# First aggregation of a graph attention layer: both outer strips of scores in one turning product, h's 64-column rests turned in pairs, the first group's h turned ahead of the next sums

## The chip, the cores and the metric

The kernel runs on one core of one Trainium2 chip. The time is device microseconds of one execution. Before the change three runs took 1733.44, 1734.93 and 1737.89 us; the median is 1734.93 us.

## What is computed

Two layers of relational graph attention over 3125 nodes and 53125 edges (sorted by their target), with 768 features; the first layer has 4 heads of 192 columns, the second one head of 768. Then a residual and a normalisation. Cut to what matters:

```python
def rgat_conv(x, W, q, k, b, src, dst, etype, heads, out_ch, n_nodes):
    xr = jnp.einsum('nd,rdf->rnf', x, W)          # 3 relations
    oi = xr[etype, dst]
    oj = xr[etype, src]
    alpha = jax.nn.leaky_relu(oi @ q + oj @ k, NEG_SLOPE)
    m = jax.ops.segment_max(alpha, dst, num_segments=n_nodes)
    e = jnp.exp(alpha - m[dst])
    z = jax.ops.segment_sum(e, dst, num_segments=n_nodes)
    a = e / (z[dst] + EPS)
    msg = (a[:, :, None] * oj.reshape(-1, heads, out_ch)).reshape(-1, heads * out_ch)
    return jax.ops.segment_sum(msg, dst, num_segments=n_nodes) + b

h = jax.nn.elu(rgat_conv(x, W1, q1, k1, b1, src, dst, edge_type, 4, 192, n))
out = rgat_conv(h, W2, q2, k2, b2, src, dst, edge_type, 1, 768, n)
x = _layernorm(x + out, axis=-1)
```

## The kernel before, in words

The work has three stages, one after another. `phase1` (with the preparation ahead of it) multiplies x by W1 for all relations and stores the rows, each with its key score, in a table in memory. `phase2` is the first aggregation: it gathers the rows of the table edge by edge, weighs and adds them per target node, makes h from the sums, multiplies h by W2 and stores the rows of the second table. `phase3` is the second aggregation over that table, with the residual and the normalisation.

Both aggregations take the nodes in 25 groups of 128. A group has 17 slots (14 in the first group) of 128 edges. One slot is one indirect DMA issued by GpSimd (`gather_rows`, L480), which brings 128 rows of 772 floats into a ring of row buffers. The slots 0 to 7 of a group are its first part (u = 0), the others its second (u = 1).

One part of a group in `phase2` runs through these steps. `alpha` (L887) adds the query and key scores of the part's slots and takes the leaky maximum into `al`, one column for each slot and head, with 128 edges down the partitions. `turn` (L898) turns these columns into rows in PSUM, three times by three products of TensorE: the slots shifted back by one, the slots themselves, the slots shifted on by one. The three strips of 128 columns stand side by side in the bank `pa`. `scan` (L906) needs the middle strip and 64 columns (`REACH`) on either side of it: two running maxima on VectorE, a difference, and an exponential on ScalarE. `back` (L919) turns the result back, `weigh` (L940) multiplies it into the selection matrices `sel`, and `sums` (L957) adds the rows by products with `sel` into two banks `acc`.

Once for each group come the steps of h. `e_y` (L1001) divides by the sum of weights and adds the bias, giving `y` (four windows of 192 columns, in a tile whose windows are 256 wide); `e_x` takes the exponential on ScalarE; `e_h` (L1051) finishes the elu in three VectorE steps, of which one puts the last 64 columns of each window a second time behind the 192, so that each window has two blocks of 128. `h_row` stores h. `e_t` (L1066) turns y by eight products into the PSUM tile `pt`: `turned(s, 0)` the first 128 columns of the four windows, `turned(s, 1)` the last 128, which hold the same 64 columns twice. `e_s` copies the high parts into `hT` on ScalarE (one copy of 512 columns, two of 256 on 64 partitions each), and `e_s2` makes the low parts on VectorE in the same pieces. `d_part` issues the 72 products of h with W2 one by one, `d_row` (L1102) copies each quarter of the result out and, after every second quarter, stores a whole row block of 386 KB.

`phase3` does the same with one head: `a_alpha` (L1294), `a_turn` (L1304, again three products), `a_scan`, and so on.

The order on every engine is written out by hand. Each step is given a place, counted in slots, by `when(place, step, ...)`, and all steps are issued in the order of their places. `STEPS2["h"]` holds the places of e_y, e_x, e_h, h_row, e_t, e_s and e_s2, `STEPS2["first"]` and `STEPS2["second"]` those of alpha, turn, scan, back, weigh and sums of the two parts. For the first group (b = 0) the base is -3, for the second 14; a group's base is that of the one before plus 17. A gather also waits for a product of the group before, by a count of TensorE cycles (`paced`, L489).

Of the kernel before, what the change touches and what calls it, by code (L numbers as in the profile page):

```python
# [21 lines left out]
P = 128  # L22
# [8 lines left out]
REACH = 64  # L31

# [32 lines left out]
def _index(ap):  # L65
# [4 lines left out]
SL = 17  # L70
# [21 lines left out]
          "h": (26.1, 26.45, 28.4, 28.5, 34.52, 34.6, 34.62),  # L92
          "d": ((37, 38.5, 16), (43.2, 45.2, 20), (45.5, 47, 16), (51.7, 53.7, 20)),
# [21 lines left out]
def kernel(  # L115
# [355 lines left out]

    W3 = P + 2 * REACH

# [365 lines left out]
    def phase2(work, psum):  # L839
# [15 lines left out]
        for t in als:  # L855
            V.memset(t, 0.0)
# [30 lines left out]
        def alpha(b, u):  # L887
            if u == 0:
                st["a", b] = work.tile([P, SL, H1], F32, name="a", bufs=2)
            a = st["a", b]  # L890
            i, e = (0, CUT + 1) if u == 0 else (CUT + 1, slots(b))
            for i_, e_, g in stretches(ring, lambda j: base(b) + j, i, e):
                key = g.rearrange("p n (h f) -> p n h f", h=H1)[:, :, :, F1]
                V.tensor_add(a[:, i_:e_], pall[:, b, i_:e_], key)
                V.memset(key, 1.0)
            V.scalar_tensor_tensor(als[b % 2][:, 1 + i:1 + e], a[:, i:e], NEG_SLOPE, a[:, i:e], op0=ALU.mult, op1=ALU.max)

        def turn(b, u):  # L898
            a, e = part(b, u)
            n = H1 * (e - a)  # L900
            pa = st["pa", b, u] = psum.tile([P, 512], F32, name=f"pa{u}", bufs=1)
            for c in range(3):
                T.transpose(pa[:n, c * P:(c + 1) * P],
                            als[b % 2][:, a + c:e + c].rearrange("p j h -> p (j h)"), ident)
# [96 lines left out]
        def e_y(b):  # L1001
# [6 lines left out]
            y = s["y"] = work.tile([P, 4, 2 * P], F32, name="y", bufs=1)  # L1008
            for w in range(4):
                V.scalar_tensor_tensor(y[:, w, :F1], acc[w // 2][:, w % 2, :F1], rz[:, w // 2, w % 2:w % 2 + 1],  # L1010
                                       bias1, op0=ALU.mult, op1=ALU.add)

        def e_x(b):
            s = blk[b]
            s["ey"] = work.tile([P, 4, F1], F32, name="ey", bufs=1)
            S.activation(s["ey"], s["y"][:, :, :F1], AF.Exp)
# [7 lines left out]
        def turned(s, c):  # L1024

            for t in range(4):
                T.transpose(s["pt"][:, c, t * P:(t + 1) * P], s["y"][:, t, c * P:(c + 1) * P], ident)

        def high_parts(s, c):
# [6 lines left out]
            for u in range(2):  # L1036
                p = slice(64 * u, 64 * u + 64)
                S.copy(hT[p, 0, H1:], pt[p, u::2])

        def low_parts(s, c):  # L1040
# [6 lines left out]
            for u in range(2):  # L1047
                p = slice(64 * u, 64 * u + 64)
                V.tensor_sub(hT[p, 1, H1:], pt[p, u::2], hT[p, 0, H1:].bitcast(F32))

        def e_h(b):  # L1051
# [3 lines left out]
            V.scalar_tensor_tensor(y[:, :, F1:], y[:, :, P:F1], 0.0, ey[:, :, P:], op0=ALU.max, op1=ALU.add)  # L1055
            V.scalar_tensor_tensor(y[:, :, :F1], y[:, :, :F1], 0.0, ey, op0=ALU.max, op1=ALU.add)

        def h_row(b):
# [4 lines left out]
            for h in range(H1):  # L1063
                nc.sync.dma_start(to[h], s["y"][32 * h:32 * h + 32, :, :F1])
# [37 lines left out]
        def d_row(b, p):  # L1102
# [5 lines left out]
            if c == 1:  # L1108
# [27 lines left out]
        for b in range(NB):  # L1136
# [14 lines left out]
            for d, f in zip(STEPS2["h"], (e_y, e_x, e_h, h_row, e_t, e_s, e_s2)):  # L1151
                when(at_0 + d, f, b)
# [22 lines left out]
    def phase3(work, psum):  # L1175
# [7 lines left out]
        for t in als:  # L1183
# [110 lines left out]
        def a_alpha(b):  # L1294
# [7 lines left out]
            V.scalar_tensor_tensor(al[:, 1:SL + 1], a, NEG_SLOPE, a, op0=ALU.mult, op1=ALU.max)  # L1302

        def a_turn(b):  # L1304
            pa = blk[b]["pa"] = psum.tile([P, 512], F32, name="pa", bufs=1)
            for c in range(3):
                T.transpose(pa[:SL, c * P:(c + 1) * P], als[b % 2][:, c:c + SL], ident)
# [892 lines left out]
```

## Time and profile before

| what | value |
| --- | --- |
| three runs | 1733.44, 1734.93, 1737.89 us |
| the profiled execution's own time | 1735.37 us |
| its span, first to last instruction | 1733.4 us |
| TensorE busy | 1643.7 us, 95% |
| weight loads | 1277.1 us, 74% |
| VectorE busy | 1075.3 us, 62% |
| ScalarE busy | 423.3 us, 24% |
| GpSimd busy | 910.8 us, 53% |
| mean granted TensorE clock | 0.977 of full speed |
| moved by DMA | 500.48 MB |

All times inside the profile are microseconds from the span's start unless they are marked ns. PE is TensorE, PEld its weight loads, DVE VectorE, ACT ScalarE, POOL GpSimd, SP SyncE; a q behind the name is the engine's own queue. L58 is the line of a helper that records every turning product and L55 that of every other product, so the tiles tell them apart: `pa` is the bank of the scores, `pt` that of h, `acc` the sums, `po` the products with W2, `hT` the turned h. In a row of the timeline the first number is the start, the second the length, and xN the number of instructions merged into it; what stands in brackets is the idle time of the engine just before and what ended it. In the chain of waits, the piece ahead of each line is what held up the work that ended last.

The first aggregation lies between about 534 and 1131 us, the second between about 1135 us and the end.

### The profile page before, as it was taken

Reading aid. Unit: us, or ns where it says so; the run is one execution under the profiler, and the core shown is the slowest. Engines: PE = TensorE matmul, PEld = TensorE weight load, DVE = VectorE, ACT = ScalarE, POOL = GpSimd, SP = SyncE. Lnnn points to the kernel's source line nnn. Section 1 sums busy time; section 2 is a strip of 40 time slices with the busy share of each in tenths; the row PEclk is TensorE's granted clock in tenths of the full one; section 3 lists DMA queues with packets and bytes.
Section 4 is the critical chain, followed back from the end, with each engine's and each line's share of the span. In section 5 each row is a group of like instructions: output and inputs, shape, how many; then the busy total and the mean of one; then the engine's idle time right before and its main releaser. Section 6 shows DMA issues by size and latency. Waiting matters only on the chain.

```text
span 1733.4 us, 39074 instructions
## 1 busy us (share of the span) xinstructions
PE 1643.7 (95%) x14308; PEld 1277.1 (74%) x14308; DVE 1075.3 (62%) x3953; ACT 423.3 (24%) x796; POOL 910.8 (53%) x907
## 2 busy tenths in 40 slices
PE   9999999999996999999999999939999999999996
PEld 8999999999995788888888888924444444444443
DVE  5467666675425556665677777455666666666665
ACT  5122222112110111111111111202333333333333
POOL 5100000000007777777777777067777777777770
PEclk9999999999997999999999999969999999999999
DMA  9676766666568999999999999579999999999990
GB/s 328 185 237 211 256 218 212 198 179 211 197 236 290 342 342 343 349 347 341 341 352 351 355 348 343 163 235 321 335 337 336 333 339 333 339 335 338 334 329 29
DMA packets 169367, 500.48 MB, mean 289 GB/s; under 512 B 39890, under 2 KB 82489, under 8 KB 169166
## 3 DMA queue, kind: packets, MB, share of 16 engines
q0 software_dynamic: 70832, 343.91, 56.1%
q1 hardware_dynamic: 90104, 143.89, 25.0%
q10 hardware_dynamic: 8230, 10.10, 1.7%
q8 instruction: 114, 1.87, 0.4%
q14 instruction: 87, 0.71, 0.1%
HBM read 412.96 MB, written 89.63 MB: 290 GB/s over the span
## 4 chain that ended last, share of the span: by engine, by line
PE 74%; DMA 11%; issue 6%; POOL 4%; DVE 3%; ACT 0%; POOLq 0%; SPq 0%; DVEq 0%; ACTq 0%
PE po L55 45%; PE acc L55 17%; PE D L55 6%; DMA waL<-ftab,ridx 3%; DMA waH<-ftab,ridx 3%; PE pa L58 2%; POOL waH L480 2%; PE pt L58 1%; DMA share<-ftab,ridx 1%; POOL waL L480 1%; DMA share<-in_w_t_dram 1%; POOL extra L480 1%; DMA extra<-ftab,rfirst 1%; DMA e<-in_edge_type_dram 1%; DMA extra<-ftab,ridx 1%
## 5 line engine op out<-in xcount | busy, mean ns | idle before, releaser
L480 POOL DMA_INDIRECT extra<-ftab,ridx x296 | 305.8, 1033 | 90.2 <-issue 53.3
L55 PE MATMUL po<-waH,hT 128*128 128x386 f32 (+1 forms) x1200 | 322.7, 344 | 1.0 <-DVE hT L1045 0.8
L55 PE MATMUL po<-waH,xT 128*128 128x386 f32 x1104 | 293.0, 341 | 0.0
L480 POOL DMA_INDIRECT share<-ftab,ridx x209 | 216.4, 1036 | 63.7 <-issue 36.6
L55 PEld LDWEIGHTS po<-waH,hT 128*128 128x128 f32 x1200 | 220.1, 189 | 3.4 <-DVE hT L1045 1.1
L55 PE MATMUL po<-waL,hT 128*128 128x386 f32 (+1 forms) x600 | 207.5, 346 | 0.0
L55 PE MATMUL D<-extra,AT 128*128 128x512 f32 (+1 forms) x576 | 203.3, 504 | 0.0
L55 PEld LDWEIGHTS po<-waH,xT 128*128 128x128 f32 x1104 | 202.5, 189 | 0.5 <-issue 0.4
L55 PE MATMUL po<-waL,xT 128*128 128x386 f32 x552 | 186.9, 339 | 0.0
L55 PEld LDWEIGHTS D<-extra,AT 128*128 128x128 f32 x576 | 108.3, 195 | 79.5 <-issue 73.5
L593 ACT COPY share<-po 128x386 f32<-128x386 f32 x150 | 72.4, 483 | 371.4 <-PE po L55 303.9
L55 PE MATMUL acc<-waL,marks 128*32 128x386 f32 (+1 forms) x860 | 151.9, 489 | 0.0
L55 PE MATMUL po<-wbH,xT 128*128 128x386 f32 (+1 forms) x552 | 147.4, 341 | 1.3 <-DVE wbL L430 1.3
L55 PE MATMUL acc<-waH,marks 128*32 128x384 f32 (+1 forms) x828 | 140.4, 493 | 0.7 <-DVE marks L1346 0.7
L55 PE MATMUL acc<-extra,marks 128*32 128x386 f32 (+1 forms) x564 | 129.5, 487 | 0.0
L480 POOL DMA_INDIRECT waL<-ftab,ridx x108 | 108.1, 1001 | 32.9 <-issue 27.4
L55 PE MATMUL acc<-extra,sel 128*32 128x193 f32 x2736 | 123.2, 332 | 2.2 <-DVE sel L953 2.2
L917 ACT ACTIVATE e<-e 32x128 f32<-32x128 f32 (+2 forms) x50 | 15.5, 310 | 436.2 <-DVE e L916 436.2
L480 POOL DMA_INDIRECT waH<-ftab,ridx x103 | 104.0, 1010 | 31.4 <-issue 26.2
L55 PEld LDWEIGHTS po<-waL,hT 128*128 128x128 f32 x600 | 113.4, 189 | 0.6 <-issue 0.3
L757 POOL DMA_DIRECT2D share<-in_L_gnn_W_dram x24 | 12.9, 538 | 188.4 <-DVE w2j L768 117.2
L55 PEld LDWEIGHTS acc<-extra,sel 128*32 128x32 f32 x2736 | 86.7, 111 | 32.0 <-issue 6.7
(302 smaller groups left out, 3045.0 us busy)
## 6 DMA issues: line engine op xcount, KB each, us to landing
ftab<-share SPq DMA_DIRECT2D x150, 193.0 KB
ftab<-r SPq DMA_DIRECT2D x50, 386.0 KB
sT<-dr_d SPq DMA_DIRECT2D x23, 544.0 KB
xb_d<-share SPq DMA_DIRECT2D x25, 384.0 KB
ftab<-y SPq DMA_DIRECT2D x100, 96.0 KB
share<-xb_d SPq DMA_DIRECT2D x25, 384.0 KB
share<-in_x_dram SPq DMA_DIRECT2D x24, 384.0 KB
out_dram<-share SPq DMA_DIRECT2D x24, 384.0 KB
```

The costliest lines, as they stand in the source:

```text
L55: return self.add(self.engine.matmul(to, weights, moving, **more), to, moving)
L58: return self.add(self.engine.transpose(to, a, unit), to, a)
L480: return G.indirect_dma_start(out=to, out_offset=None, in_=tab, in_offset=_index(i[:, j:j + 1]), bounds_check=NP * R - 1, oob_is_err=False)
L593: S.copy(o[:, :HW], po[:, :HW])
L757: G.dma_start(w2[i][p:p + n], l2["W"][r, at:at + n, :])
L917: S.activation(e, e, AF.Exp)
```

## The change

In both aggregations the two outer strips are made by one turning product in place of two. A new tile (`near`, in the second aggregation `next_to`) gets, by two VectorE copies of 64 partitions each, the edges 0 to 63 of the next slot and the edges 64 to 127 of the slot before; its product writes two blocks of 64 columns to either side of the middle strip, through the view `sides`. `alpha` and `a_alpha` gain the two copies, `turn` and `a_turn` have two products in place of three.

The last 64 columns of h's windows go into a tile of their own, `rest`, four times 64 columns, and are turned two windows at a time: two products in place of four. `y` has windows of 192 columns with no gap. `e_s` and `e_s2` take the rests in four pieces of 128 columns on 64 partitions in place of two of 256.

The first group has its own places, `h0`: e_h 0.08 of a slot earlier, e_t, e_s and e_s2 1.32 to 1.38 slots earlier. In the last group `d_row` stores each quarter by itself.

```diff
+    def sides(pa):
+        return pa[:, P - REACH:P - REACH + 2 * (P + REACH)].rearrange("n (s f) -> n s f", s=2)[:, ::-1, :REACH]
...
           "h": (26.1, 26.45, 28.4, 28.5, 34.52, 34.6, 34.62),
+          "h0": (26.1, 26.45, 28.32, 28.5, 33.2, 33.22, 33.24),
...
+            al, to = als[b % 2], near[b % 2]
+            n = max(i, 1)
+            V.tensor_copy(to[:REACH, n - 1:e - 1], al[:REACH, 1 + n:1 + e])
+            n = min(e, SL - 1)
+            V.tensor_copy(to[P - REACH:, 1 + i:1 + n], al[P - REACH:, 1 + i:1 + n])
 
         def turn(b, u):
...
-            for c in range(3):
-                T.transpose(pa[:n, c * P:(c + 1) * P],
-                            als[b % 2][:, a + c:e + c].rearrange("p j h -> p (j h)"), ident)
+            T.transpose(pa[:n, P:2 * P], als[b % 2][:, 1 + a:1 + e].rearrange("p j h -> p (j h)"), ident)
+            T.transpose(sides(pa[:n]), near[b % 2][:, a:e].rearrange("p j h -> p (j h)"), ident)
...
-            for t in range(4):
-                T.transpose(s["pt"][:, c, t * P:(t + 1) * P], s["y"][:, t, c * P:(c + 1) * P], ident)
+            if c == 0:
+                for t in range(4):
+                    T.transpose(s["pt"][:, 0, t * P:(t + 1) * P], s["y"][:, t, :P], ident)
+                return
+            for t in range(2):
+                T.transpose(s["pt"][:, 1, t * P:(t + 1) * P], s["rest"][:, t * P:(t + 1) * P], ident)
+
+        def rests(s, k):
+            hT = s["hT"].rearrange("p s t (m q i) -> p s t m q i", q=2, i=32)
+            pt = s["pt"][:, 1, :2 * P].rearrange("p (m t u i) -> p t m u i", m=2, u=2, i=32)
+            for u in range(2):
+                for q in range(2):
+                    yield hT[64 * u:64 * u + 64, k, H1:, :, q], pt[64 * q:64 * q + 64, :, :, u]
...
-            for u in range(2):
-                p = slice(64 * u, 64 * u + 64)
-                S.copy(hT[p, 0, H1:], pt[p, u::2])
+            for to, rest in rests(s, 0):
+                S.copy(to, rest)
...
-            for u in range(2):
-                p = slice(64 * u, 64 * u + 64)
-                V.tensor_sub(hT[p, 1, H1:], pt[p, u::2], hT[p, 0, H1:].bitcast(F32))
+            for (to, rest), (high, _) in zip(rests(s, 1), rests(s, 0)):
+                V.tensor_sub(to, rest, high.bitcast(F32))
...
-            V.scalar_tensor_tensor(y[:, :, F1:], y[:, :, P:F1], 0.0, ey[:, :, P:], op0=ALU.max, op1=ALU.add)
-            V.scalar_tensor_tensor(y[:, :, :F1], y[:, :, :F1], 0.0, ey, op0=ALU.max, op1=ALU.add)
+            V.scalar_tensor_tensor(s["rest"].rearrange("p (w f) -> p w f", w=4), y[:, :, P:], 0.0, ey[:, :, P:], op0=ALU.max, op1=ALU.add)
+            V.scalar_tensor_tensor(y, y, 0.0, ey, op0=ALU.max, op1=ALU.add)
...
-            if c == 1:
+            if b == NB - 1:
+                f = slice(c * HW, (c + 1) * HW)
+                nc.sync.dma_start(s["rows"][:, r, f], rows[r][:, f])
+            elif c == 1:
                 nc.sync.dma_start(s["rows"][:, r, :], rows[r])
...
-            for d, f in zip(STEPS2["h"], (e_y, e_x, e_h, h_row, e_t, e_s, e_s2)):
+            for d, f in zip(STEPS2["h" if b else "h0"], (e_y, e_x, e_h, h_row, e_t, e_s, e_s2)):
...
+            V.tensor_copy(next_to[b % 2][:REACH, :SL - 1], al[:REACH, 2:SL + 1])
+            V.tensor_copy(next_to[b % 2][P - REACH:, 1:], al[P - REACH:, 1:SL])
...
-            for c in range(3):
-                T.transpose(pa[:SL, c * P:(c + 1) * P], als[b % 2][:, c:c + SL], ident)
+            T.transpose(pa[:SL, P:2 * P], als[b % 2][:, 1:SL + 1], ident)
+            T.transpose(sides(pa[:SL]), next_to[b % 2], ident)
```

More of the change, by code (lines that the diff above doesn't have):

```diff
@@ L31 @@
 REACH = 64
+assert 2 * REACH == P
 GRP = 8
@@ L854, in phase2 @@
         als = [work.tile([P, SL + 2, H1], F32, name=f"al{i}", bufs=1) for i in range(2)]
-        for t in als:
+        near = [work.tile([P, SL, H1], F32, name=f"near{i}", bufs=1) for i in range(2)]
+        for t in als + near:
             V.memset(t, 0.0)
@@ L1007, in e_y @@
             V.reciprocal(rz, rz)
-            y = s["y"] = work.tile([P, 4, 2 * P], F32, name="y", bufs=1)
+            y = s["y"] = work.tile([P, 4, F1], F32, name="y", bufs=1)
+            s["rest"] = work.tile([P, 2 * P], F32, name="rest", bufs=1)
             for w in range(4):
-                V.scalar_tensor_tensor(y[:, w, :F1], acc[w // 2][:, w % 2, :F1], rz[:, w // 2, w % 2:w % 2 + 1],
+                V.scalar_tensor_tensor(y[:, w], acc[w // 2][:, w % 2, :F1], rz[:, w // 2, w % 2:w % 2 + 1],
                                        bias1, op0=ALU.mult, op1=ALU.add)
@@ L1015, in e_x @@
             s["ey"] = work.tile([P, 4, F1], F32, name="ey", bufs=1)
-            S.activation(s["ey"], s["y"][:, :, :F1], AF.Exp)
+            S.activation(s["ey"], s["y"], AF.Exp)
         def busy(n):
@@ L1063, in h_row @@
             for h in range(H1):
-                nc.sync.dma_start(to[h], s["y"][32 * h:32 * h + 32, :, :F1])
+                nc.sync.dma_start(to[h], s["y"][32 * h:32 * h + 32])
         def e_t(b):
@@ L1182, in phase3 @@
         als = [work.tile([P, SL + 3], F32, name=f"al2_{i}", bufs=1) for i in range(2)]
-        for t in als:
+        next_to = [work.tile([P, SL], F32, name=f"next{i}", bufs=1) for i in range(2)]
+        for t in als + next_to:
             V.memset(t, 0.0)
```

## Prediction

> **What bounds the kernel now.** I read the page first, then the busy time by stretches, the chain of waits, the waits of TensorE, and the timelines of single engines.
>
> ```profile
> PE 1643.7 (95%) x14308; PEld 1277.1 (74%) x14308; DVE 1075.3 (62%) x3953; ACT 423.3 (24%) x796; POOL 910.8 (53%) x907
> ```
>
> 95% is an average over stages, so the stages are looked at one by one. First one group of the first aggregation. Columns: stretch, length, busy time (and instructions) of PE, PEld, DVE, ACT, POOL, granted clock, DMA share, GB/s.
>
> ```profile
> 850.40:873.40 23.00, 23.00 (x276) 19.86 (x280) 15.12 (x48) 4.26 (x10) 17.81 (x18) 1.00 0.98 343
> ```
>
> TensorE has no gap and the full clock; the waits of TensorE between 600 and 1080 us list nothing. The chain of waits gives the period, from the second part's sums of two groups:
>
> ```profile
> 597.36 4.38 PE acc L55 x104
> ...
> 1103.32 4.38 PE acc L55 x104
> ```
>
> 22 groups lie between them: (1103.32 - 597.36) / 22 = 23.00 us each. The second aggregation's gathers, the first and the last of 422:
>
> ```profile
> 1135.47 1.21 POOL L480 DMA_INDIRECT waH<-ftab,rfirst  x1 [47.49 <-DMA f<-ed_d]
> 1687.27 1.00 POOL L480 DMA_INDIRECT share<-ftab,ridx  x1 [0.30 <-issue]
> ```
>
> 421 steps in 551.8 us are 1.31 us each, which is one gather (1.00) and its issue (0.30 to 0.31) with next to nothing between. So the first aggregation lasts as long as TensorE's work, and the second starts when the first ends and then lasts as long as GpSimd issues gathers.
>
> **Turning products.** TensorE at the two places in a group where parts are turned:
>
> ```profile
> 854.71 0.50 PE L58 MATMUL pa<-fident,al 128*32 128x128 f32 x3
> ...
> 865.28 0.50 PE L58 MATMUL pa<-fident,al 128*36 128x128 f32 x3
> 865.62 1.04 PE L58 MATMUL pt<-fident,y 128*128 128x128 f32 x8
> 866.41 0.42 PE L55 MATMUL po<-waL,hT 128*128 128x386 f32 x1
> ```
>
> Starts count here, not lengths, since products overlap. Three products on `al` take 865.62 - 865.28 = 0.34 us, 0.113 each; eight on y take 866.41 - 865.62 = 0.79, 0.099 each. A group loses two of the first kind (one in each part) and two of the second: 0.226 + 0.198 = 0.42 us. The new product writes two blocks of 64 columns, a shape that no row shows; I take the price of one plain product, since it moves as many columns. Cheaper it could only be by the 0.113 itself; as two pieces of 0.113 it would take back that edit's gain. From 578 to 1131 us 46 parts and 24 groups' y are turned: 46 x 0.113 + 48 x 0.099 = 9.9 us, if nothing else becomes late.
>
> **What is late next: the gathered rows.** VectorE's `alpha` waits for them, and the turning products wait for `alpha`.
>
> ```profile
> 601.14 0.18 DVE L896 SCALAR_TENSOR_TENSOR al<-a 128x36 f32<-128x36 f32 x1
> 601.67 0.50 PE L58 MATMUL pa<-fident,al 128*32 128x128 f32 x3
> ...
> 876.88 0.22 DVE L894 TENSOR_TENSOR a<-pall,share 128x32 f32<-128x32 f32 x1 [1.61 <-DMA share<-ftab,ridx]
> 877.17 0.16 DVE L896 SCALAR_TENSOR_TENSOR al<-a 128x36 f32<-128x36 f32 x1
> 877.70 0.50 PE L58 MATMUL pa<-fident,al 128*32 128x128 f32 x3
> ...
> 1083.11 0.18 DVE L896 SCALAR_TENSOR_TENSOR al<-a 128x36 f32<-128x36 f32 x1
> 1084.63 0.50 PE L58 MATMUL pa<-fident,al 128*32 128x128 f32 x3
> ```
>
> The first part's `al` is ready 0.35 us ahead of its turning at 601 and 0.37 at 877; over the 13 groups from the one to the other it is 0.15 to 0.87, 0.57 in the mean. The change draws on this twice. Two copies come between `al` and the turning product: 0 to 0.18 us each, by the step before them, and the first waits for that step's result; 0.1 to 0.4 together, I take 0.25, the middle. And TensorE comes 0.31 us sooner (one strip and two y products lie between the point that sets the gathers' pace and this turning). Taking 0.56 from each of the 13 leaves six below zero, 1.4 us in sum. Behind the product that then waits a group's 20 `po` products are queued, so such a wait is the path's.
>
> What sets the gathers' pace, VectorE first, then GpSimd:
>
> ```profile
> 860.42 0.55 DVE L1053 TENSOR_SCALAR ey<-ey 128x768 f32<-128x768 f32 x1
> 861.01 0.42 DVE L1055 SCALAR_TENSOR_TENSOR y<-y,ey 128x256 f32<-128x256 f32 x1
> 861.47 0.96 DVE L1056 SCALAR_TENSOR_TENSOR y<-y,ey 128x768 f32<-128x768 f32 x1
> ...
> 861.54 1.75 POOL L480 DMA_INDIRECT share<-ftab,ridx  x1 [0.30 <-PE po L55]
> 863.60 1.00 POOL L480 DMA_INDIRECT share<-ftab,ridx  x1 [0.30 <-DVE moved L986]
> ...
> 1086.98 1.00 POOL L480 DMA_INDIRECT share<-ftab,ridx  x1 [0.30 <-issue]
> ```
>
> The gather that begins under `e_h`'s last step ends 0.86 us after it, 0.75 late. 17 gathers and their issue are 22.2 us, with this one hold 23.0: it ties the gathers to TensorE's period, and at 22.58 us need only be 0.4 long. From 863.60 on the steps that move the index hold gathers too: 166 gathers in 223.38 us are 22.88 us a group. Against 22.58 they lose 0.30 a group. The slack there (1.34 us at 1084), less 0.56, carries about three of ten groups; seven lose 0.30, 2.1 us. The first aggregation keeps 9.9 - 1.4 - 2.1 = 6.4 us.
>
> The Trainium skill ("SBUF — State Buffer", "Who interferes with whom") says that a VectorE copy can enter a mode that takes the port pair shared with GpSimd, and that whichever of the two comes second is blocked for the whole instruction. The held gather agrees in kind; no run here shows it of such copies. By the rows alone the copies hold nothing and the sum stands; by the rule at its full reach it would be that of the slower rival below.
>
> **h's high and low parts.** ScalarE, VectorE, and TensorE's first use:
>
> ```profile
> 868.18 0.74 ACT L1038 CAST hT<-pt 64x256 fp32r<-64x256 f32 x2
> 868.95 0.69 DVE L1045 TENSOR_TENSOR hT<-pt,hT 128x512 fp32r<-128x512 f32 x1 [1.55 <-ACT hT L1038]
> 869.56 0.85 DVE L1049 TENSOR_TENSOR hT<-pt,hT 64x256 fp32r<-64x256 f32 x2
> 870.29 0.44 PE L55 MATMUL po<-waH,hT 128*128 128x386 f32 x1
> ```
>
> Four pieces of half the size cost between the same and double, 0.74 to 1.48 and 0.85 to 1.70; I take 1.1 on both, nearer the same. The first low part, which waits for all the high ones, ends at 869.64 and would come 0.36 later; TensorE needs it 0.31 sooner, with the third product, a little after 870.29. Of 0.7 us or more of cover some remains. It costs nothing, at the dear end about 0.4 a group.
>
> **The first group.** e_h moves ahead of the next group's `weigh` on VectorE; the turning of y, and its split on ScalarE and VectorE, ahead of that group's sums. GpSimd's queue has one gather between, which waits for none of this; SP's has nothing. (The row from 572 is one of stretches; its clock is 0.50.)
>
> ```profile
> 559.15 0.84 ACT L1016 ACTIVATE ey<-y 128x768 f32<-128x768 f32 x1 [1.41 <-DVE y L1010]
> 559.03 1.54 DVE L953 TENSOR_TENSOR sel<-marks,pa 128x1024 f32<-128x1024 f32 x2
> 560.29 5.46 PE L55 MATMUL acc<-extra,sel 128*32 128x193 f32 x80 [2.19 <-DVE sel L953]
> 570.11 0.62 PE L55 MATMUL po<-waH,hT 128*128 128x386 f32 x2 [0.75 <-DVE hT L1045]
> 572.00:574.00 2.00, 2.00 (x7) 1.56 (x5) 1.97 (x10) 0.00 (x0) 1.70 (x2) 0.50 0.91 358
> 574.01 1.14 PE L55 MATMUL acc<-extra,sel 128*32 128x193 f32 x16
> ```
>
> This is a new wait: VectorE stands until ScalarE's exponential ends at 559.99, then does e_h's three steps, to 562.0. `sel` is queued behind it and the sums wait for `sel`, so they come 2.9 us later, at 563.2. They take 5.5 us as before, or 3.4 at the second part's full pace (80 of 104 in 4.38). In return the products that stood until 570.11, 4.4 us after the sums, no longer wait for the split: 0.74 + 0.69 us less, 2.9 after. They are 16, at half clock 4.5 us (14 took 3.9), at full clock 2.3. The next sums begin between 571.8 and 576.1, against 574.01; I take no change, the middle.
>
> **The end of the stage, and the rest.**
>
> ```profile
> 1131.92 2.60 DMA ftab<-r
> ```
>
> The last store, on which the second aggregation's gathers wait, is halved: 0 to 1.3 us less, I take 0.5, nearer to a fixed price as no split store is shown. The copies on the path at the start and in the last groups cost 0.3 (0.25 less one strip, each), and 50 of them beside the second aggregation's gathers another 0.3: +0.6. One strip less in each group there gives nothing, as GpSimd sets its length.
>
> **Sum.** -6.4 - 0.5 + 0.6 = -6.3 us. The profiled execution took 1735.4, so 1729.1; the median of the runs is 0.4 below that execution: 1728.7.
>
> **Rivals.**
> 1. The whole 9.9 us arrives, because the landings come sooner too (for it: 1.34 us of slack at 1084; against: six of 13 slacks below zero): -9.9 - 0.5 + 0.6, 1725.2. Chance 0.19.
> 2. The landings set the period and it stays at 23.0 (for it: DMA share 0.98; against: GpSimd's 22.2): +0.1, 1735.1. Chance 0.16.
> 3. The two blocks of 64 cost two products, so that edit does not do what it says: 5.2 us go, and most of the waits with them; 1730.9. Chance 0.1.
> 4. Slower: each copy holds a gather for its length. Its place is the second aggregation, where GpSimd has no cover: 50 x 0.18 = 9 us; in the first, four copies a group bring the gathers to 22.9, so 2 of the 9.9 remain. 1742. It decides from 0.13 us per copy, where 50 of them eat 6.5. Against it: 421 steps there hold only 2.4 us in all beyond 1.305 each. Chance 0.05.
>
> The forecast has 0.50. A measurement of this kernel can tell about 0.3%, 5.2 us, from no change, so faster begins below 1729.7: some 0.37 of the forecast and rival 1, 0.56. Slower is rival 4, 0.05; the same 0.39. The range, 1724.0 to 1733.8, goes a little below rival 1 and takes in rival 3 and the dear ends of the forecast; it leaves out rivals 2 and 4, 0.2.
>
> **What would show it.** Right: 22.6 to 22.8 us between the sums; two `pa` and six `pt` products at 0.10 to 0.11 from start to start; waits of TensorE at `pa` for VectorE's copies, 0.1 to 0.3 a group; the second aggregation's gathers 551 to 553 us from first to last; a last store under 2.6. A period of 22.58 without such waits is rival 1, one of 23.0 rival 2, 0.2 us behind the new product rival 3, long gathers beside copies rival 4. I am wrong if the period falls and the time does not.

## The result, and the profile after

Nine runs of the changed kernel took 1730.03 us in the median (1727.71 to 1733.77), nine runs of the kernel before beside them 1735.03 (1733.44 to 1738.55). The ratio is 0.9969 (95% interval 0.9960 to 0.9979): 5.0 us less, where 6.3 were forecast. The profiled execution took 1729.88 us, its span is 1728.1.

The page of the changed kernel, the line of busy times:

```profile
PE 1636.1 (95%) x14183; PEld 1266.2 (73%) x14183; DVE 1113.7 (64%) x4157; ACT 431.5 (25%) x846; POOL 906.0 (52%) x907
```

TensorE has 125 recorded products and 7.6 us less, VectorE 204 instructions and 38.4 us more. What that is worth shows only stage by stage. First the two turning places of one group on TensorE, for which the starts count:

```profile
853.17 0.28 PE L59 MATMUL pa<-fident,al 128*32 128x128 f32 x1
853.29 0.27 PE L59 MATMUL pa<-fident,near 128*32 128x128 f32 x1
...
863.66 0.29 PE L59 MATMUL pa<-fident,al 128*36 128x128 f32 x1
863.79 0.27 PE L59 MATMUL pa<-fident,near 128*36 128x128 f32 x1
863.90 0.60 PE L59 MATMUL pt<-fident,y 128*128 128x128 f32 x4
864.33 0.38 PE L59 MATMUL pt<-fident,rest 128*128 128x128 f32 x2
864.47 0.42 PE L56 MATMUL po<-waL,hT 128*128 128x386 f32 x1
```

The product of the two blocks of 64 columns takes 0.11 us (863.79 to 863.90), as much as a plain one, and the whole place 0.81 us where it took 1.13. Now the chain of waits, sums of the second part, four groups in a row:

```profile
848.85 4.38 PE acc L56 x104
871.46 4.38 PE acc L56 x104
894.01 4.38 PE acc L56 x104
917.12 4.55 PE acc L56 x104
```

The period is 22.61 and 22.55 us: 0.42 less than the 23.00 of before, to the digit of the forecast. The last one is 23.11, and its sums take 4.55 us in place of 4.38. Such longer periods are the largest part of the difference between the 9.9 us that the products gave and the 5.0 that came. The waits of TensorE between 600 and 1130 us (total, times, longest), name some of them (the list counts only idle stretches of over 0.15 us); before the change this list is empty:

```profile
PE pa L59 <- DVE al L903: 2.1, 4, 0.9
PE acc L56 <- DVE sel L964: 1.5, 3, 0.5
PE pa L59 <- DVE near L908: 0.3, 1, 0.3
```

Shorter waits for the copies show only from start to start. Where the scores came late, as at the longest of these waits, the product on `near` follows the one on `al` after 0.31 us in place of 0.12:

```profile
762.68 0.27 PE L59 MATMUL pa<-fident,al 128*32 128x128 f32 x1 [0.86 <-DVE al L903]
762.99 0.28 PE L59 MATMUL pa<-fident,near 128*32 128x128 f32 x1
```

Between group 3 and group 24 this happens at six turnings of first parts, 0.20 to 0.55 us each, together 1.3 us more than 0.12 each.

The end of the stage, from the chain of waits, and the first and the last of the second aggregation's 422 gathers:

```profile
1128.88 1.87 DMA ftab<-r
```

```profile
1131.53 0.99 POOL L486 DMA_INDIRECT waH<-ftab,rfirst  x1 [45.09 <-DMA ftab<-r]
...
1681.05 1.00 POOL L486 DMA_INDIRECT share<-ftab,ridx  x1 [0.30 <-issue]
```

The last store takes 1.87 us in place of 2.60, the second aggregation begins 3.9 us sooner (1.0 of it because group 0 was turned that much sooner in this execution), and its gathers take 549.5 us from first to last (551.8 before).

For all kernels below I use one table. It cuts the profiled execution at the turning of the first part of group 0, of group 3 and of group 24, at the first gather of the second aggregation, and at the last one (us; each number is the difference of two starts in the timeline).

| kernel | group 0 to 3 | 3 to 24 | 24 to first gather | these three | gathers |
| --- | --- | --- | --- | --- | --- |
| before | 61.1 | 483.0 | 50.8 | 594.9 | 551.8 |
| before, second profile | 62.0 | 483.6 | 50.9 | 596.5 | 550.2 |
| after | 62.6 | 480.1 | 49.3 | 592.0 | 549.5 |
| after, second profile | 65.1 | 476.3 | 49.3 | 590.6 | 549.8 |
| e_h in four | 62.9 | 476.8 | 49.3 | 589.0 | 548.9 |
| first part turned later | 65.3 | 479.2 | 48.4 | 592.8 | 551.2 |
| first h not ahead | 61.4 | 477.1 | 49.3 | 587.7 | 549.1 |
| three mends | 61.3 | 474.7 | 49.3 | 585.3 | 549.9 |
| strips alone | 61.6 | 481.0 | 50.6 | 593.3 | 551.1 |
| rests alone | 62.0 | 481.5 | 50.5 | 593.9 | 551.2 |

From group 3 to group 24 are 21 groups; at 22.57 us, the mean of the undisturbed ones, they take 474.0. The profile of after lies 6.1 us above that, its second profile 2.3. The two profiles of one kernel differ by 1.4 to 1.6 us over the three stretches, so smaller differences between kernels can't be read from this table.

### The profile page after: what moved, and what is told of

Same layout as the page of the kernel before. It is cut to its first block, busy times and chain, and to the rows that moved or that the text cites. A ratio compares the mean times of both kernels' runs of the same rounds, so it can differ in the third digit from the quotient of the medians.

```text
span 1728.1 us, 39081 instructions
## 1 busy us (share of the span) xinstructions
PE 1636.1 (95%) x14183; PEld 1266.2 (73%) x14183; DVE 1113.7 (64%) x4157; ACT 431.5 (25%) x846; POOL 906.0 (52%) x907
## 4 chain that ended last, share of the span: by engine, by line
PE 68%; DMA 13%; issue 7%; DVE 6%; POOL 4%; ACT 0%; POOLq 0%; DVEq 0%; ACTq 0%; SPq 0%
PE po L56 44%; PE acc L56 13%; PE D L56 6%; DMA extra<-ftab,ridx 4%; DMA waL<-ftab,ridx 2%; DMA share<-ftab,ridx 2%; PE pa L59 2%; DMA waH<-ftab,ridx 2%; POOL waH L486 2%; PE pt L59 1%; DMA spare_rows<-ftab,ridx 1%; POOL waL L486 1%; POOL extra L486 1%; POOL share L486 1%; DVE marks L1374 1%
## 5 line engine op out<-in xcount | busy, mean ns | idle before, releaser
L56 PE MATMUL acc<-share,marks 128*32 128x384 f32 (+1 forms) x456 | 109.7, 487 | 0.0
## 6 DMA issues: line engine op xcount, KB each, us to landing
sT<-dr_d SPq DMA_DIRECT2D x23, 544.0 KB
```

The source lines that it names most:

```text
L56: return self.add(self.engine.matmul(to, weights, moving, **more), to, moving)
```

## The experiments

**On a slower chip.** The first four kernels ran on another chip, on which the kernel before takes 1948.32 us (1947.35 to 1952.82). My theory A was that the step of e_h that holds a gather ties the gathers to TensorE's pace; B that the rows land late because the DMA queues are full; C that the copies of the scores cost what is missing.

e_h's last step in four:

```diff
-            V.scalar_tensor_tensor(y, y, 0.0, ey, op0=ALU.max, op1=ALU.add)
+            for w in range(4):
+                V.scalar_tensor_tensor(y[:, w], y[:, w], 0.0, ey[:, w], op0=ALU.max, op1=ALU.add)
```

> The changed kernel with e_h's last step (0.96 us) cut into four steps of one window each. Theory A (the gathers run at TensorE's pace because that step holds one of them until it ends, so a group that comes sooner gets its rows no sooner): holds of at most 0.3 us, the gathers run ahead, 22.5 to 22.7 us from one first-part turning to the next in nearly all groups, waits of TensorE in groups 3 to 24 of 2 us or less against 7.7 us in the changed kernel, 1724 to 1726.5 us. Theory B (the DMA queues are full, the rows land late whatever GpSimd does): waits stay at 5 to 8 us, 1729 to 1731. Theory C (the new copies cost the time, by their length or by holding gathers): no change, 1729 to 1731, with long gathers beside the copies.

Measured: 1964.80 us, ratio 1.0085 (1.0067 to 1.0102).

The rows of h not stored, x's rows copied into the table during the first stage:

```diff
+            if b < NB - 1:
+                return
             for h in range(H1):
                 nc.sync.dma_start(to[h], s["y"][32 * h:32 * h + 32])
```

> The changed kernel without the stores of h's rows in the first aggregation (384 KB of some 7.8 MB a group; x's rows stand in the table in their place, copied during the first stage). Theory B: 5% less to move, the DMA share falls to about 0.93, the landings come sooner, waits of 2 us or less, 1724 to 1727. Theories A and C: waits stay at 5 to 8 us, 1728.5 to 1731.

Measured: 1963.76 us, ratio 1.0079 (1.0065 to 1.0093).

Only the strips of scores, in both aggregations, with their copies; the rest as before:

```diff
-            for c in range(3):
-                T.transpose(pa[:n, c * P:(c + 1) * P], ...)
+            T.transpose(pa[:n, P:2 * P], als[b % 2][:, 1 + a:1 + e].rearrange("p j h -> p (j h)"), ident)
+            T.transpose(sides(pa[:n]), near[b % 2][:, a:e].rearrange("p j h -> p (j h)"), ident)
...
```

> Only the turning products of the scores are changed (both aggregations, with the copies); h's rests, the first group's places and the stores are those of before. Theories A and B: a saving of 0.226 us a group draws little on the slack, waits of 1 to 2 us, 1730.5 to 1732.5. Theory C: the copies eat the saving, 1734 to 1736.

Measured: 1958.37 us, ratio 1.0048 (1.0034 to 1.0062).

Only h's rests; the scores, the places and the stores as before:

```diff
-                T.transpose(s["pt"][:, c, t * P:(t + 1) * P], s["y"][:, t, c * P:(c + 1) * P], ident)
+            for t in range(2):
+                T.transpose(s["pt"][:, 1, t * P:(t + 1) * P], s["rest"][:, t * P:(t + 1) * P], ident)
...
```

> Only h's rests are changed (two products fewer a group, four half-size pieces in place of two); scores, places and stores are those of before, no copies. Theories A and B: 0.2 us a group, nearly all kept, 1730.5 to 1732. Theory C: the same, and all that the whole change gains, 1729.5 to 1731, while the strips alone gain nothing.

Measured: 1958.79 us, ratio 1.0052 (1.0038 to 1.0066).

Here nothing could be told apart, because another thing sets the time. Busy time by stretches on this chip, e_h in four, and below it the same kernel on a chip on which the kernel before takes 1736 us (PE, PEld, DVE, ACT, POOL, clock, DMA share, GB/s):

```profile
660.00:860.00 200.00, 185.48 (x1997) 152.69 (x1987) 112.57 (x388) 34.36 (x92) 127.81 (x127) 1.00 0.91 298
```

```profile
660.00:860.00 200.00, 200.00 (x2398) 172.06 (x2396) 135.77 (x470) 40.02 (x106) 153.96 (x152) 1.00 0.98 354
```

TensorE has the full clock on both, but stands for 14.5 of 200 us on the slower chip, and 298 GB/s are moved in place of 354. There a group takes 26.6 us (turning at 812.77, next at 839.41), far above the 22.57 of TensorE's products. What TensorE waits for in this stretch the profile doesn't name; most of it stands under "issue", which means that it waited for nothing that the profile shows:

```profile
PE acc L56 <- issue: 9.9, 27, 1.1
```

That gathered rows set the pace there is argued from the lower rate and not shown. What is shown is that the two parts of the change gained nothing there. Why the four were slower than before by 0.5 to 0.9% was not settled: neither a profile of the kernel before nor a run of the changed kernel was taken on that chip.

**The same chip as before and after.** The next eight ran on chips on which the kernel before takes 1734.6 to 1736.0 us in the median.

The kernel before, for a second profile:

> The kernel before, unchanged, for a profile of it on this chip. Where before takes about 1735 us, all theories expect the period of a group in the first aggregation at 22.98 to 23.00 us, as on record. On a chip where it takes about 1948 us: if rows that land late set the pace there (B), the period is 26 us or more, TensorE is busy for under 92% of 660:860, and TensorE's waits for the gathered scores (al) and sums are spread over nearly every group; if TensorE is throttled there (rival D), it is busy for over 98% at a granted clock well below 0.97.

Measured: 1734.49 us in one run. The period from group 3 to 24 is 22.96 to 23.00, but for one of 23.77.

The changed kernel again:

> The kernel after, unchanged. Where before takes about 1735 us: 0.9969 of it (0.996 to 0.998) by all theories. Where before takes about 1948 us: the two runs of one part each took 1.0048 and 1.0052 of before there. If what slows them is one common cause (a TensorE that is done sooner stands and waits for rows, and the rows come no sooner), after is 1.003 to 1.007 of before; if each part brings a cost of its own, the costs add and after is 1.009 to 1.011.

Measured: 1730.17 us (1729.17 to 1735.11), ratio 0.9970 (0.9958 to 0.9982). Its profile differs from the first in one thing that helped me most: it loses the time at other places. From group 4 to 16 every period is 22.54 to 22.61, with no wait; in return it took 27.4 us from group 2 to group 3. TensorE at that place:

```profile
585.76 3.12 PE L56 MATMUL acc<-extra,sel 128*32 128x193 f32 x72
591.58 0.29 PE L59 MATMUL pa<-fident,al 128*36 128x128 f32 x1 [2.69 <-DVE al L903]
```

and the busy time by stretches around it:

```profile
586.00:589.00 3.00, 2.88 (x72) 2.00 (x64) 0.54 (x5) 0.00 (x0) 2.38 (x3) 1.00 1.02 287
592.50:596.00 3.50, 3.50 (x14) 3.50 (x13) 1.55 (x4) 1.97 (x7) 2.79 (x3) 0.51 1.04 408
596.00:600.00 4.00, 4.00 (x24) 3.71 (x23) 3.31 (x8) 0.71 (x2) 3.09 (x4) 1.00 1.00 380
```

With a wait of 2.69 us for rows this group takes 4.8 us more than 22.57. After the wait the granted clock is 0.51 for some 3.5 us: 14 products are done in 3.5 us, where the next 4 us hold 24. At half clock 3.5 us lose about 1.7 (an estimate from this row); the small rest goes to two products on `near` that come late. In the first profile TensorE waits 0.93 us at the same place and keeps the full clock (1.00 from 590 to 594). The Trainium skill ("TensorE: Matmul & The Clock Gate", "What's actually happening") says that the clock is halved after an idle window of about 3.4 us and given back after a busy one of the same length, and that these windows run freely, whatever the kernel does. The trace agrees in the half clock and its length, but the wait that brought it was 2.69 us, shorter than such a window.

Why are rows late there? Two rows of GpSimd, first profile of after, show a part of it, and beside them TensorE:

```profile
559.74 1.00 POOL L486 DMA_INDIRECT share<-ftab,rfirst  x1 [0.30 <-issue]
562.47 1.00 POOL L486 DMA_INDIRECT share<-ftab,rfirst  x1 [1.74 <-PE pt L59]
```

```profile
556.85 0.24 PE L59 MATMUL pa<-fident,e 32*128 32x32 f32 x1 [2.13 <-ACT e L928]
561.30 1.11 PE L59 MATMUL pt<-fident,y 128*128 128x128 f32 x4 [4.20 <-DVE y L1078]
```

TensorE stands 4.20 us for the first group's y, and ahead of a gather, which `paced` ties to a product of TensorE, GpSimd stands 1.74 us (2.40 in the second profile) until y has been turned, where 0.30 is usual. The gathers behind it run at 1.30 us each without a pause, so they can't make it good. The time is lost either in one wait (second profile) or bit by bit up to group 11 (first profile, where the periods lie between 22.6 and 24.1 until there). How much of it the held gather explains differs. The last gather of group 2 is issued 43.8 us after group 0's turning in the first profile and 42.9 in the second, against 42.3 with the early turning undone (below), and the scores take up its rows 6.0, 7.7 and 5.9 us after that. So in the first profile the lateness is the hold; in the second most of it lies in the landing, and why that took longer is open.

e_h in four on this chip:

> After, with e_h's last step in four steps of a window each. Theory A (a gather that falls beside that 0.96 us step is held for 0.75 us until it ends, which ties the gathers to TensorE's pace and eats the slack in groups whose gathers have slipped): the holds of 0.78 us become 0.2 or less, the period floor of the gathers falls from 22.58 to 22.4, the long periods (23.0 to 24.1) go and some 4 to 6 us are gained on after: 1724 to 1727 where before takes 1735. Theory B (rows land late because the queues are full): the holds become shorter too, but the long periods stay and the time is within 1.5 us of after. Theory C (the copies themselves cost it): the same as B. On a chip where before takes 1948 us all three expect after within 0.3%.

Measured: 1727.39 us (1725.62 to 1730.71), ratio 0.9946 (0.9933 to 0.9959). The step that held a gather, VectorE and GpSimd of after (second profile):

```profile
929.51 0.96 DVE L1078 SCALAR_TENSOR_TENSOR y<-y,ey 128x768 f32<-128x768 f32 x1
```

```profile
929.58 1.77 POOL L486 DMA_INDIRECT share<-ftab,ridx  x1 [0.30 <-DVE rest L1077]
```

and with the step in four:

```profile
932.23 1.17 DVE L1079 SCALAR_TENSOR_TENSOR y<-y,ey 128x192 f32<-128x192 f32 x4
```

```profile
932.29 1.18 POOL L486 DMA_INDIRECT share<-ftab,ridx  x1 [0.30 <-DVE rest L1077]
```

The hold falls from 0.77 to 0.18 us: a gather that begins beside this step waits until the one VectorE instruction is done. The Trainium skill ("SBUF — State Buffer", "Who interferes with whom") says that a VectorE instruction with two inputs in SBUF contends with a GpSimd instruction that reads SBUF; y and ey are such inputs, the gather reads its row numbers there, and the 0.77 us agree. Theory A expected more: that the long periods go with the holds. Three periods are still 23.3, in groups 16, 18 and 20, so the holds do not make these, and theory A falls for them. For the long periods ahead of group 11 the run decides nothing: from group 3 to 24 the kernel takes 476.8 us, and after takes 480.1 in one profile and 476.3 in the other. The median is 2.8 us below that of after, more than theories B and C allow and a little less than A gave; the profiled execution was the slowest of the five, so where the 2.8 us lie isn't shown, and the intervals touch.

The first part's turning, scan, back and weights 0.6 slot later:

```diff
-          "first": (8.4, 9, 9.05, 11.3, 11.35, 17.4),
+          "first": (8.4, 9.6, 9.65, 11.9, 11.95, 17.4),
```

> After, with turn, scan, back and weights of a group's first slots put 0.6 slot (0.79 us) later among the products, their scores and copies where they are. All waits of TensorE at pa for the scores of the first part (5.6 us in the profile of after) are bought off if the rows are late by less than 0.79 us at that place. Theory A: the lateness is a matter of 0.3 to 0.8 us (a hold of 0.78 and the copies' 0.4), so most of the waits go, 3 to 5 us are gained on after: 1725 to 1727 where before takes 1735. Theory B: the gathers have no rate to spare, TensorE comes sooner at the next place where it waits (sums for rows, the second part), and the time is within 1.5 us of after. Theory C: within 1 us of after, since the copies cost the same wherever they lie. On a chip where before takes 1948 us: within 0.3% of after by B; up to 0.5% faster by A.

Measured: 1734.88 us (1730.33 to 1741.14), ratio 0.9992 (0.9981 to 1.0004): 4.7 us slower than after, against all three theories. The waits of TensorE between 600 and 1130 us:

```profile
PE acc L56 <- DVE sel L964: 3.0, 7, 0.6
```

The waits for scores are gone from this stretch, as they should be, and the waits for `sel` have become seven. Three belong to second parts, in groups 16, 18 and 20, as in after. Four are new and belong to first parts, whose weights this edit put 0.79 us later: it traded waits for rows for waits on VectorE. Of the 4.7 us the three stretches of the table show 0.8 to 2.2. (The expectation's 5.6 us counts the start and the second parts too; between 600 and 1130 us after waits 2.4 for scores.) What the run points to is VectorE's work ahead of `weigh`.

This led to theory M. VectorE and TensorE around the second part's weights in group 16, before (second profile):

```profile
915.85 0.85 DVE L1049 TENSOR_TENSOR hT<-pt,hT 64x256 fp32r<-64x256 f32 x2
916.73 0.50 DVE L992 TENSOR_SCALAR pall<-ridx,first_row,moved 128x425 f32<-128x425 int32 x1
917.27 0.60 DVE L993 TENSOR_TENSOR pall<-pall 128x425 f32<-128x425 f32 x1
917.90 2.02 DVE L953 TENSOR_TENSOR sel<-marks,pa 128x1152 f32<-128x1152 f32 x3
```

and after (second profile), VectorE, then TensorE:

```profile
913.92 1.18 DVE L1071 TENSOR_TENSOR hT<-pt,hT 64x128 fp32r<-64x128 f32 x4
915.13 0.50 DVE L1003 TENSOR_SCALAR pall<-ridx,first_row,moved 128x425 f32<-128x425 int32 x1
915.67 0.60 DVE L1004 TENSOR_TENSOR pall<-pall 128x425 f32<-128x425 f32 x1
916.31 2.02 DVE L964 TENSOR_TENSOR sel<-marks,pa 128x1152 f32<-128x1152 f32 x3
```

```profile
917.72 4.22 PE L56 MATMUL acc<-share,sel 128*32 128x193 f32 x96 [0.51 <-DVE sel L964]
```

Count from the part's turning, which is at 911.57 before and at 909.41 after:

```profile
911.57 0.50 PE L58 MATMUL pa<-fident,al 128*36 128x128 f32 x3
...
919.62 4.13 PE L55 MATMUL acc<-share,sel 128*32 128x193 f32 x96
```

```profile
909.41 0.29 PE L59 MATMUL pa<-fident,al 128*36 128x128 f32 x1
```

The weights begin 6.33 us behind it before and 6.90 after: the four pieces cost 0.33 us more on VectorE, and the rest is their high parts on ScalarE, which take 1.07 us in place of 0.74. The sums are due 8.05 us behind the turning before, and only 7.80 after (917.72 less the wait). In most groups there is room for that. In groups 16, 18 and 20 a step of `move` (1.1 us) stands between, and TensorE waits 0.5 us; with the slower sums behind the wait a period of 23.28 comes out, 0.71 more than 22.57. Three of them are 2.1 us.

The first group's h not turned ahead:

```diff
-            for d, f in zip(STEPS2["h" if b else "h0"], (e_y, e_x, e_h, h_row, e_t, e_s, e_s2)):
+            for d, f in zip(STEPS2["h"], (e_y, e_x, e_h, h_row, e_t, e_s, e_s2)):
```

> After, with the first group's h turned at the same place as the others' (that part undone). In the three profiles with the part, TensorE stands 3.5 to 4.2 us at pt for y of the first group, one gather of that stretch is held 1.7 to 2.4 us until the turning, and from group 0's turn to group 3's it takes 62.6, 65.1 and 62.9 us; before takes 62.0. Theory S (the part costs at the start: the held gather makes the rows of groups 2 and 3 late): the held gather goes, the stretch becomes 60.5 to 62.0 us, and the time is 1 to 3 us below after (1727 to 1729 where after takes 1730). Theory N (the rows of the first groups set the stretch with or without it): the wait at pt turns into one at al, the stretch stays at 62 to 65 us and the time within 1 us of after. Theory G (the part gains the 2.2 us that it was meant for): 2 us above after. On a chip where before takes about 1948 us: all within 0.3% of after.

Measured: 1726.53 us (1724.41 to 1728.00), ratio 0.9949 (0.9934 to 0.9964), on a chip where the kernel before takes 1734.63 us. The gather at that place, GpSimd:

```profile
559.29 1.05 POOL L486 DMA_INDIRECT share<-ftab,rfirst  x1 [0.31 <-issue]
560.65 1.00 POOL L486 DMA_INDIRECT share<-ftab,rfirst  x1 [0.30 <-PE acc L56]
```

No gather is held there, the stretch from group 0 to 3 takes 61.4 us in place of 62.6 and 65.1, and the three stretches together 2.9 and 4.3 us less than in the two profiles of after. Theory S holds in kind: this part of the change cost about 3 us, 3.6 between the medians where S gave 1 to 3. Not all long periods of the start go: groups 3 and 5 take 23.0 us here too.

All three mends (e_h in four, first h not ahead, and a new one). The new one keeps `move` out of the stretch ahead of the second part's weights, and also out of the one ahead of the first part's (7 to 12.2):

```diff
-            when(base(late) + STEPS2["move"] + i * (NB - 1 - late) * SL / (NB - 2), move, i + 1)
+            k = base(late) + STEPS2["move"] + i * (NB - 1 - late) * SL / (NB - 2)
+            p = (k - base(late)) % SL
+            for lo, hi in ((-3, 2.87), (7, 12.2), (14, SL + 2.87)):
+                if lo <= p < hi:
+                    k += hi - p
+                    break
+            when(k, move, i + 1)
```

> After with three edits: e_h's last step in four, the first group's h not turned ahead, and the steps of move kept out of the stretch between the low parts of h's rests and the second part's weights. Theory M (the rests' eight pieces put VectorE 0.56 us later before the weights, and where a move of 1.1 us falls there too, in groups 16, 18 and 20, TensorE waits 0.5 us for sel and runs slower for a moment: 0.72 us each): the three periods of 23.3 us become 22.6 and 2.1 us are gained; with 2.8 us of e_h in four (measured) and 1 to 3 us of the start by theory S, 1722 to 1725 us where after takes 1730. Rival R (what is saved at one place comes back as a wait for rows at the next): 1726 to 1728, with the periods of groups 16 to 21 still over 23 us, ended by a wait for al in place of sel. Rival C (the copies of the scores are what is left): the same as R with waits for near.

Measured: 1725.06 us (1721.79 to 1727.27), ratio 0.9937 (0.9920 to 0.9954), the fastest of all. VectorE in group 16, then the chain of waits for the sums of groups 15 to 17:

```profile
913.76 1.19 DVE L1071 TENSOR_TENSOR hT<-pt,hT 64x128 fp32r<-64x128 f32 x4
914.98 2.02 DVE L964 TENSOR_TENSOR sel<-marks,pa 128x1152 f32<-128x1152 f32 x3
916.91 0.50 DVE L1003 TENSOR_SCALAR pall<-ridx,first_row,moved 128x425 f32<-128x425 int32 x1
```

```profile
894.37 4.38 PE acc L56 x104
...
917.04 4.38 PE acc L56 x104
...
939.59 4.38 PE acc L56 x104
```

The weights come first, no wait for `sel` is left in these groups, and from group 3 to 24 it takes 474.7 us: 0.7 above what the products alone need, and 2.4 less than the kernel with the first h not ahead and nothing else mended. Theory M holds by the trace. The medians of these two kernels differ by 1.5 us with overlapping intervals, which by themselves would not show it. Nor do the mends add up in the medians: 2.8, 3.6 and the 2.1 of theory M are 8.5 us, and 5.1 came. (In this profiled execution, as in that of e_h in four, one of the first loads landed about 2 us later, and group 0 was turned at 544.0 and 545.0 us, in the others of the table between 539.4 and 542.0; the stretches of the table are free of that.)

The strips alone and the rests alone, with the edits of the third and fourth kernel, on a chip where the kernel before takes 1735.84 us:

> Before, with the outer strips of scores in one product (both aggregations, copies too) and nothing else of the change. Theory T (TensorE's products set the group: its period in before is 22.99 us with TensorE busy 199.96 of 200 us): two products of 0.113 us less are 0.226 a group, the period becomes 22.77 us, and 24 groups give 5.4 us: 1728.5 to 1731 where before takes 1734.6 to 1736. Theory H (17 gathers of 1.303 us and a hold of 0.77 beside e_h's step are 22.9 to 23.0 us, so that the gathers keep the old period until two savings together move them to another place): the period stays at 22.9 to 23.0 with the hold of 0.77 in most groups, and the time is 1732.5 to 1735. On a chip where before takes about 1948 us: 1.003 to 1.006 of before, as it was there.

Measured: 1732.33 us (1728.63 to 1737.41), ratio 0.9977 (0.9964 to 0.9990). From group 10 on the periods are 22.75 to 22.82 but for one, as theory T has it. Ahead of that several are 22.98 to 23.15, and one is 24.00. A hold of 0.6 to 0.8 us stands in nearly every group up to group 14, also beside periods of 22.8, so it does not keep the old period as H has it. The time is 1.3 us above what T gave, because of the periods ahead of group 10, which no run explains.

> Before, with h's 64-column rests turned in pairs (and their copies in eight pieces) and nothing else of the change. Theory T: two products of 0.099 us less are 0.198 a group, a period of 22.79 us and 4.7 us less, but three periods of the second half (groups 16, 18, 20) with a wait for sel of 0.3 to 0.5 us, 0.4 to 0.7 us each: 1731 to 1732.5 where before takes 1734.6 to 1736. Theory H: the period stays at 22.9 to 23.0 and the time is 1733.5 to 1736. If the waits for sel do not come here, it is not the rests' pieces that put VectorE late but the strips' copies. On a chip where before takes about 1948 us: 1.003 to 1.007 of before.

Measured: 1735.41 us (1732.58 to 1738.07), ratio 0.9994 (0.9983 to 1.0005). The waits of TensorE between 600 and 1130 us:

```profile
PE acc L56 <- DVE sel L960: 1.5, 3, 0.5
PE pa L59 <- DVE al L903: 0.7, 1, 0.7
```

The period is 22.79 as in theory T, and for groups 16, 18 and 20 it is 23.48 (23.61 for group 22, which ends in the one wait for scores): the wait for `sel` comes with the rests, without any copy of scores, and the strips alone have none. So it is the eight pieces that make VectorE late. The time was 3 us above what T gave and inside what H gave, with a period that H does not have. Its three stretches are 1.0 and 2.6 us shorter than those of the two profiles of before, and 0.4 arrives in the median; the runs scatter by 5 us, and what took the rest is open. The two parts alone give 3.9 us together, and the kernel with both, with the last stores split and without the early turning 8.1, on another chip; with intervals of 2 to 3 us to either side of each, I can't say whether there is more in it than scatter.

## Why the prediction held, and where it did not

The time came out 1.3 us above the forecast and inside its range, on the side forecast. By its own steps:

- **A group loses 0.42 us of TensorE.** Right: 23.00 became 22.57. The product of two blocks of 64 costs one product (0.11 us), which ends rival 3. A period of 23.0 throughout (rival 2) isn't there either.
- **Waits for rows, 3.5 us.** The sum was right for the one execution, by luck; the cause only in part. Of the 6.1 us above the products' own time from group 3 to 24, 2.1 are waits for `sel` and 4.0 are late scores; in the second profile late scores take 0.2 there, since that execution had lost its time ahead of group 3. The first term, 1.4 us for rows and copies that use up a slack of 0.57 us, is there in kind: the copies end 0.40 us behind `al` (forecast 0.25), and TensorE loses 1.3 us on them at six turnings of the first profile. But with the early turning undone a group's scores are ready 0.3 to 1.9 us ahead of the turning from group 7 on, copies and all. The second term, 2.1 us for gathers that `move` holds in seven groups behind 863, is not there: behind group 14 the first profile has one wait for scores (0.66 us, and 0.28 for the copies behind it), the second none.
- **h's high and low parts, nothing.** Here a step failed. Their price was right (1.07 us on ScalarE and 1.18 on VectorE, forecast 1.1). Their cover was sought at the products that read them, where no wait shows. What stands behind them on VectorE was left out: the second part's weights, 0.57 us later where the sums are due 0.25 sooner, and in three groups a step of `move` between. 2.1 us, shown by the rests alone (the waits come) and by the three mends (they go).
- **The first group, nothing, between -2.2 and +2.1.** The step that failed is the sentence that GpSimd has one gather there "which waits for none of this". It waits for the turning, since `paced` ties it to a product of TensorE, and moving the turning ahead put a product that waits for y in front of it. GpSimd stands 1.74 to 2.40 us ahead of it, and the part costs about 3 us: more than the dear end. Undoing it gave 3.6 us between the medians. That the gather is held is shown; that this alone makes the cost is shown for the first profile only, as said above.
- **The last store, -0.5.** It was -0.7 (2.60 to 1.87).
- **The copies elsewhere, +0.6.** At the start they are seen: in groups 0 to 2 of the first profile `near` follows `al` after 0.31 to 0.46 us at four turnings, 1.1 us more than 0.12 each. In the second aggregation they are not. Its gathers take 549.5 us in place of the 551 to 553 forecast, and the nine of them that begin while a copy runs take 1.00 us each, as the others do. So these copies hold no gather and rival 4 is out: the blocking by a copy that the Trainium skill ("SBUF — State Buffer", "Who interferes with whom") says can happen does not show here. The strips alone, with copies, take 551.1 us there and the rests alone, without, 551.2. Whether the 1 to 2 us less than before are a gain isn't settled, as two profiles of before differ by 1.6.

So the sum was near because errors met: about 5 us of cost that the forecast did not have (first group, `sel`), against rows that cost less than 3.5 us once these two are away, an end of the stage that came 1.5 us sooner and not 0.5 (0.4 of it the last group's own products, which are in the 9.9), and a second aggregation that did not pay for its copies. Where the gain lies also changes from one execution to the next: in the first pair of profiles the three stretches of the first aggregation give 2.9 of 5.3 us, in the second pair 5.9 of 5.1. So that the time came out within 1.3 us of the forecast is in part luck. Rival 1, the whole 9.9 us, was not far from what the change can give: without the early turning it takes 1726.5 us, and 1725.1 with the two further edits that the change does not have.

## What to carry to other kernels

When a step is moved ahead on one engine, look for every instruction of other queues that is tied to its place, pacing waits too: a step that stands there now makes them stand. When a step becomes longer, price not only the reader of its result but the next thing on its own engine, and look for the groups in which something else falls between. And where TensorE is the bound by a hair, the last half microsecond of each group is decided by the slowest of the others: take the profile a second time before a wait is blamed, since the same kernel lost its time at two different places.

## What the runs showed of the hardware

A wait of TensorE of 2.69 us was followed by about 3.5 us at a granted clock of 0.51, and its group took 4.8 us more; a wait of 0.93 us at the same place left the clock at 1.00. One wait is in both profiles of the changed kernel, 1.97 us long, in group 0: in the first the clock is 0.50 behind it (545.9 to 549.2), in the second 1.00 (545.7 to 550). So the length of a wait alone does not decide. Even a wait of 0.51 us was followed by 104 products in 4.55 us in place of 4.38.

A VectorE step on two SBUF operands holds an indirect gather that begins beside it until it ends: 0.77 us for a step of 0.96, 0.18 for its quarter of 0.29. A copy of scores on 64 partitions (0.17 us) does not: gathers that begin beside one take 1.00 us.

The kernel before takes 1735 us on some chips and 1948 on another. With e_h in four, a stretch of the first aggregation moves 298 GB/s there in place of 354, at the same full TensorE clock. On that chip fewer products of TensorE gave nothing.
